# Conditional residual layer: W1 of the first eight batches loaded by id, and the row copies moved behind the first product

## The chip, the cores and the metric

The kernel runs on one core of one Trainium2 chip. The metric is device time in microseconds (us) of one execution. Before the change it is 313.89 us, the median of three runs (313.76 to 314.14). The trace used below is of one profiled execution, which took 313.83 us.

## The reference, cut to what matters

There are 128 batches of x, each 128 rows of 512 float32 values. Each batch has an integer id from 0 to 8 that picks one of ten sets of parameters.

```python
w1 = W1[ids]                 # (512, 128) per batch
w2 = W2[ids]                 # (128, 512) per batch
h = relu(einsum('bsh,bha->bsa', x, w1) + b1[ids][:, None, :])
y = x + einsum('bsa,bah->bsh', h, w2) + b2[ids][:, None, :]
out = x + layernorm(y) * gamma[ids][:, None, :] + beta[ids][:, None, :]
```

W1 is (10, 512, 128), W2 is (10, 128, 512); b1 is (10, 128), b2, gamma and beta are (10, 512).

## The kernel before, in words

One batch is one tile of 128 partitions by 512 columns. Four batches share one buffer of x (512 columns each, `xp`, four buffers). For each batch b:

- `transpose_x(b)` (L211, PE): four 128x128 transposes of x into one PSUM tile `pxT` (a single buffer); `copy_xT(b)` (L220, ACT) copies it to SBUF. For b below `EARLY` (16) the transposes read every fourth column of x, because the W1 that goes with them is laid out by `(p k)`; from batch 16 on they read 128 neighbouring columns.
- `stage_w1(b)` (L206, ACT): copies the 128x512 slice of W1 that belongs to the batch's id out of the whole table in SBUF (`w1e` for b below `EARLY`, `w1` after) into a small tile `w1s` (three buffers).
- `down(b)` (L237, PE): four products of `xT` and `w1s`, accumulated in one PSUM tile `ph` (a single buffer); `relu(b)` (L247, ACT) adds b1 and makes `hT`.
- `up(b)` (L251, PE): `hT` times the id's slice of `w2`, 128x512, into `py`; the first four batches and some later ones add b2 here by one more product. `py` shares five PSUM buffers with the `row` tiles of `spread`.
- On POOL `add_b2(b)` (L224) makes x + b2 and `add_beta(b)` (L230) makes x + beta, in buffers `r` (four) and `o` (five, two batches each). On DVE and ACT follow the residual with its sum, the squares, the deviation and its reciprocal, `scale` (L319) and `finish` (L327). `store` (L334) writes two batches of `o` at once.

Before the loop come the tables. The rows of beta, gamma and b2 (30 in all) are brought to all 128 partitions: `parts` on DVE (L153 to L157) splits them in three bf16 parts, and `spread(r, copier)` (L171) does for row r one bf16 product on PE into a `row` tile and one 128x512 copy into SBUF on ACT or DVE. In the kernel before, rows 0 to 19 are spread ahead of the first `down`, in between the transposes of batches 0 and 1, and rows 20 to 29 behind `down(0)` to `down(3)`. `spin` (L451) is PE work without use: eleven products at the start, one half-width product for every second row in `spread_turn`, three before the first `down`.

The order within every engine is the order in which the program text issues, because `keep` (L44) ties each instruction to the one before it on its engine. All loads and all stores but three small ones are issued from SP's queue, in this order before the loop: ids, gamma, x of batches 0 and 1, `w1e` in two halves (L102), x of 2 and 3, `w2` in two halves (L116), x of 4 and 5, x of 6 and 7, x of 8 to 11. In the loop (`for i in range(3, B + U)`, L492), turn i issues `transpose_x(i)`, `down(i-1)`, `copy_xT(i)`, `stage_w1(i+1)`, `relu(i-1)`, `up(i-2)`, then DVE's work on batch b = i-3. The second layout of W1 (`load_w1`, L109, rows of 512 bytes) is loaded in turns 4, 6, 8 and 10. Each DMA carries one of eight semaphores in turn, and waits until the DMA eight places earlier has landed.

The id is read from `lang`, a row of 128 clamped ids that DVE makes (L147 to L150): `lid(b, engine)` (L185) loads four of them into registers of an engine.

Of the kernel before, what the change touches and what calls it, by code (L numbers as in the profile page):

```python
# [8 lines left out]
FP = mybir.dt.float32  # L9
# [4 lines left out]
ET = mybir.EngineType  # L14
PSUM = bass.MemoryType.PSUM

P = 128
G = 4
EPS = 1e-5
EARLY = 16  # L20
U = 2


# [1 line left out]
def cond_resid_kernel(ctx: ExitStack, tc: tile.TileContext, x, itok, W1, b1, W2, b2, gamma, beta, out):  # L25
# [8 lines left out]
    nc = tc.nc  # L34
    B, S, H = x.shape
    L, _, A = W1.shape
    KC = H // P
# [6 lines left out]
    def keep(ins):  # L44

        engine = ins.ins.engine
        if engine in last:
            tc.add_manual_dep(ins.ins, last[engine], behind, reason="kept order")
        last[engine] = ins.ins.name
        return ins  # L50

    const = ctx.enter_context(tc.tile_pool(name="const", bufs=1))
    xp = ctx.enter_context(tc.tile_pool(name="xp", bufs=4))
    rp = ctx.enter_context(tc.tile_pool(name="rp", bufs=4))
    op = ctx.enter_context(tc.tile_pool(name="op", bufs=5))
    tp = ctx.enter_context(tc.tile_pool(name="tp", bufs=2))
    wp = ctx.enter_context(tc.tile_pool(name="wp", bufs=3))
    st = ctx.enter_context(tc.tile_pool(name="st", bufs=6))
    p_x = ctx.enter_context(tc.tile_pool(name="p_x", bufs=1, space=PSUM))
    p_h = ctx.enter_context(tc.tile_pool(name="p_h", bufs=1, space=PSUM))  # L60
# [3 lines left out]
    xs = {}  # L64

    def load_x(g):
        t = xp.tile([P, G, H], FP, tag="x", name=f"x_{g}")
        keep(nc.sync.dma_start(out=t, in_=x[g * G : (g + 1) * G].rearrange("b s h -> s b h")))
        xs[g] = t

    def xb(b):
        return xs[b // G][:, b % G, :]
# [6 lines left out]
    w1e = const.tile([P, L, KC, A], FP, name="w1e")  # L79
    w2 = const.tile([P, L * H], FP, name="w2")  # L80
# [3 lines left out]
    def load_part(lo, hi):  # L84
        dst = xs[lo // G][:, lo % G : lo % G + hi - lo, :]
        keep(nc.sync.dma_start(out=dst, in_=x[lo:hi].rearrange("b s h -> s b h")))
# [8 lines left out]
    warm = const.tile([P, 1], FP, name="warm")  # L95
    keep(nc.vector.memset(warm, 1.0))
    keep(nc.scalar.activation(warm, warm, AF.Sqrt))


    for l in range(0, L, 5):  # L100
        keep(
            nc.sync.dma_start(  # L102
                out=w1e[:, l : l + 5].rearrange("p l k a -> p l (k a)"),
                in_=W1[l : l + 5].rearrange("l (p k) a -> p l (k a)", k=KC),
            )
        )
    load_part(2, G)

    def load_w1(k):  # L109
        keep(  # L110
            nc.sync.dma_start(out=w1[:, :, k, :], in_=W1[:, k * P : (k + 1) * P, :].rearrange("l p a -> p l a"))
        )

    for l in range(0, L, 5):
        keep(
            nc.sync.dma_start(  # L116
                out=w2[:, l * H : (l + 5) * H].rearrange("p (l h) -> p l h", l=5),
                in_=W2[l : l + 5].rearrange("l a h -> a l h"),
            )
        )  # L120
    x_1 = xp.tile([P, G, H], FP, tag="x", name="x_1")
    xs[1] = x_1
    load_part(G, G + 2)
    load_part(G + 2, 2 * G)
    load_x(2)

    ident = const.tile([P, P], FP, name="ident")
    make_identity(nc, ident)
# [7 lines left out]
    R = 3 * L  # L136
# [5 lines left out]
    keep(nc.vector.tensor_tensor(pick, both, ident[:96, 64 : 64 + R], ALU.add))  # L142
    keep(nc.vector.tensor_scalar(pick[:, L : 2 * L], pick[:, L : 2 * L], 2.0, None, ALU.mult))


    wrap = const.tile([1, B], I32, name="wrap")
    keep(nc.vector.tensor_scalar(wrap, ids, 0, L, ALU.is_lt, ALU.mult))  # L147
    lang = const.tile([1, B], I32, name="lang")
    keep(nc.vector.tensor_tensor(lang, ids, wrap, ALU.add))
    keep(nc.vector.tensor_scalar(lang, lang, 0, L - 1, ALU.max, ALU.min))  # L150

    left = rp.tile([P, H], FP, tag="r", name="left")
    keep(nc.vector.tensor_copy(parts[0:R, :], rows[0:R, :]))  # L153
# [17 lines left out]
    def spread(r, copier):  # L171
        t = (beta_b, gamma_b, b2_b)[r // L]
        row = p_y.tile([P, H], FP, tag="y", name=f"row_{r}")
        pick_r = pick[:, r : r + 1].to_broadcast([96, P])
        keep(nc.tensor.matmul(row, lhsT=pick_r, rhs=parts[:96, :], start=True, stop=True))  # L175
        dst = t[:, r % L * H : (r % L + 1) * H]
        if copier is nc.scalar:
            keep(nc.scalar.copy(dst, row))  # L178
        else:
            keep(nc.vector.tensor_copy(dst, row))  # L180

    lids, xT, w1s, hT, rs, os, ys, ssqs, nmeans, rstds = {}, {}, {}, {}, {}, {}, {}, {}, {}, {}
    phs, pxs, sums = {}, {}, {}

    def lid(b, engine):  # L185
        g = b // G
        if (g, engine) not in lids:
            loads, vals = nc.values_load_multi_w_load_instructions(
                lang[0:1, g * G : (g + 1) * G],
                engines=[engine],  # L190
                min_val=0,
                max_val=L - 1,
                skip_runtime_bounds_check_because="clamped on the chip to 0..L-1 above",
            )
            for ins in loads:
                keep(ins)
            lids[g, engine] = vals
        return lids[g, engine][b % G]

    def b2_by_matmul(b):  # L200
        return b < 4 or (b % 4 == 1 and not b2_by_vector(b))
# [4 lines left out]
    def stage_w1(b):  # L206
        w1s[b] = wp.tile([P, KC, A], FP, tag="w1s", name=f"w1s_{b}")
        src = (w1e if b < EARLY else w1).rearrange("p l k a -> p (l k a)")[:, bass.ds(lid(b, ET.Activation) * (KC * A), KC * A)]
        keep(nc.scalar.copy(w1s[b].rearrange("p k a -> p (k a)"), src))  # L209

    def transpose_x(b):  # L211
        pxs[b] = p_x.tile([P, KC, P], FP, tag="xT", name=f"pxT_{b}")
        for k in range(KC):
            if b < EARLY:
                cols = xb(b).rearrange("s (p k) -> s k p", k=KC)[:, k, :]
# [122 lines left out]
    def on(b):  # L338
        return 0 <= b < B
# [111 lines left out]
    def spin(n, width):  # L451
        idle = p_s.tile([P, H], FP, tag="s", name="idle")
        for _ in range(n):
            keep(
                nc.tensor.matmul(
                    idle[:, :width], lhsT=ones, rhs=ones[:, 0:1].to_broadcast([P, width]), start=True, stop=True
                )
            )


    def spread_turn(lo, hi):
        for r in range(lo, hi):
            spread(r, nc.scalar if r % 2 == 1 else nc.vector)
            if r % 2 == 1:
                spin(1, H // 2)

    spin(11, H)
    spread_turn(0, 2)
    transpose_x(0)
    transpose_b1()  # L470
    copy_xT(0)
    spread_turn(2, 8)
    transpose_x(1)
    copy_xT(1)
    spread_turn(8, 20)
    stage_w1(0)
    stage_w1(1)
    spin(3, H)
    for b in range(4):
        down(b)  # L480
        if b < 2:
            transpose_x(b + 2)
        relu(b)
        if b < 2:
            copy_xT(b + 2)
        for r in range(20 + 3 * b, min(23 + 3 * b, R)):
            spread(r, nc.scalar if r % 3 == 1 else nc.vector)
        stage_w1(b + 2)
    up(0)
    up(1)  # L490

    for i in range(3, B + U):  # L492
        b = i - U - 1
        if b > 0 and b % G == 0 and b // G + 3 < NG:
            load_x(b // G + 3)
        if i == 5:
            load_x(3)
        if i in (4, 6, 8, 10):
            load_w1((i - 4) // 2)
        if i == 4:  # L500
            up(2)
        if i == 5:
            up(3)
        if i > 3 and on(i):
            transpose_x(i)
        if b <= E:
            add_b2(b + 2)
            add_beta(b)
        if i > 4 and on(i - 1):
            down(i - 1)  # L510
        if i > 3 and on(i):
            copy_xT(i)
        if i > 4 and on(i + 1):
            stage_w1(i + 1)
        if i > 4 and on(i - 1):
            relu(i - 1)
        if i > 5 and on(i - U):
            up(i - U)


        g, half = divmod(b, 2)
        p = g - 1
        mine, old = 0 <= p < B // 2, 0 <= p - 1 < B // 2
        if b == E:
            add_b2(b + 3)
            add_beta(b + 1)
            add_b2(b + 4)
            for n in range(b + 2, B):
                add_beta(n)
        if b > E:  # L530
            tail(b)
        elif half == 0:
            if on(b):
                residual(b)
            if mine:
                rstd_1(p)
                scale(2 * p)
            if on(b):
                negative_mean(b)
            if mine:  # L540
                rstd_2(p)
            if old:
                finish(2 * p - 1)
                store(p - 1)
            if mine:
                rstd_3(p)
        else:
            if on(b):
                residual(b)
            if mine:  # L550
                rstd_4(p)
                scale(2 * p + 1)
            if on(b):
                negative_mean(b)
            if mine:
                finish(2 * p)
        if 0 <= b <= E:
            square(b)
            if half == 1:
                deviation(g)  # L560

        for n, engine in ((i + 3, ET.Activation), (i - U + 3, ET.PE), (b + 1, ET.DVE), (b + 5, ET.Pool)):
            if on(n):
                lid(n, engine)
# [37 lines left out]
```

## Time and profile before

| what | value |
|---|---|
| median of three runs | 313.89 us |
| the profiled execution | 313.83 us |
| span of its trace | 312.1 us |
| PE, DVE, ACT, POOL busy in the span | 300.5, 297.3, 285.4, 280.1 us |
| first `down` starts | 14.04 us |
| last product ends | about 302.3 us |
| moved by DMA | 75.49 MB, mean 242 GB/s |

The span is the time from the first to the last recorded instruction; 1.73 us of the execution lie around it. In a timeline each line has a start, a length, the engine, the line of the program, the operation with the tile written and the tile read, and how many instructions were merged; a bracket gives the idle time of the engine before it and what ended it. In a table of windows each engine has its busy time in that stretch and the number of its instructions, then come the clock granted to PE, the share of the DMA engines and what they moved. The chain of waits is followed back from the last instruction, each step to what released it.

### The profile page before, as it was taken

The page shows a single profiled execution, that of the slowest core. Times are in us where ns is not written, and L with a number is a line of the kernel's source. Part 1 is how long each engine was busy: PE and PEld are TensorE (multiplying, and loading weights), DVE is VectorE, ACT ScalarE, POOL GpSimd, SP SyncE. Part 2 cuts the span into 40 slices and gives each one's busy share as a digit, 9 for nine tenths or more (in the row PEclk, how much of TensorE's full clock was granted, in tenths as well). Part 3 has the DMA queues.
Part 4 walks back from the last instruction along what each step waited for, and adds up shares of the span by engine and source line. Part 5 has one row for each costly group of instructions (what it writes and reads, how often), then busy time and mean ns, then how long its engine had stood idle before and what let it go on. Part 6 is the DMA issues. An engine that isn't in the chain of part 4 may idle for free.

```text
span 312.1 us, 7096 instructions
## 1 busy us (share of the span) xinstructions
PE 300.5 (96%) x1869; PEld 223.8 (72%) x1869; DVE 297.3 (95%) x945; ACT 285.4 (91%) x724; POOL 280.1 (90%) x234
## 2 busy tenths in 40 slices
PE   8999999999999999999999999999999999999970
PEld 3567787777777767777777777777777777777740
DVE  6677999999999999999999999999999999999995
ACT  3878999999999999999999999999999999999982
POOL 1319978999999999999999999999999999999963
PEclk9999999999999999999999999999999999999995
DMA  6999998767776777667666567576666667633234
GB/s 209 387 387 352 326 339 275 238 229 226 236 250 225 255 265 269 242 231 270 257 227 226 210 238 253 213 272 269 232 232 198 232 247 239 244 134 138 88 149 168
DMA packets 42313, 75.49 MB, mean 242 GB/s; under 512 B 1785, under 2 KB 6916, under 8 KB 42274
## 3 DMA queue, kind: packets, MB, share of 16 engines
q1 hardware_dynamic: 42214, 75.00, 68.6%
q8 instruction: 15, 0.25, 0.3%
q14 instruction: 24, 0.20, 0.2%
q10 hardware_dynamic: 60, 0.05, 0.1%
HBM read 41.49 MB, written 33.55 MB: 240 GB/s over the span
## 4 chain that ended last, share of the span: by engine, by line
PE 91%; DVE 5%; ACT 1%; issue 1%; DVEq 1%; DMA 1%; ACTq 0%
PE ph L241 36%; PE py L258 34%; PE pxT L218 18%; PE py L257 1%; PE row L175 1%; DVE py L273 1%; DVE gamma_b L180 1%; DVE py L322 1%; DVE o L331 1%; DMA rows<-in_L_cond_b_dram 1%; ACT sq L366 0%; DVEq L597 0%; ACT n L382 0%; DVE left L156 0%; DVE left L154 0%
## 5 line engine op out<-in xcount | busy, mean ns | idle before, releaser
L235 POOL TENSOR_TENSOR o<-x,beta_b 128x512 f32<-128x512 f32 x128 | 161.6, 1274 | 12.8 <-ACT beta_b L178 9.2
L241 PE MATMUL ph<-xT,w1s 128*128 128x128 f32 x1024 | 135.6, 275 | 0.5 <-ACT w1s L209 0.5
L258 PE MATMUL py<-w,hT 128*128 x256 | 131.1, 594 | 0.0
L228 POOL TENSOR_TENSOR r<-x,b_b 128x512 f32<-128x512 f32 x93 | 118.5, 1274 | 11.5 <-DMA x<-in_x_dram 9.2
L241 PEld LDWEIGHTS ph<-xT,w1s 128*128 128x128 f32 x1024 | 124.7, 192 | 2.4 <-ACT w1s L209 1.0
L218 PEld LDWEIGHTS pxT<-ident,x 128*128 128x128 f32 x512 | 65.5, 148 | 64.9 <-issue 44.8
L322 DVE SCALAR_TENSOR_TENSOR py<-py,nmean,gamma_b 128x512 f32<-128x512 f32 x126 | 93.8, 745 | 0.2 <-issue 0.2
L331 DVE SCALAR_TENSOR_TENSOR o<-py,rstd,o 128x512 f32<-128x512 f32 x122 | 91.0, 746 | 0.0
L288 ACT ACTIVATE sq<-py,sum 128x512 f32<-128x512 f32 x124 | 85.3, 688 | 1.4 <-DVE py L273 1.3
L222 ACT COPY xT<-pxT 128x512 f32<-128x512 f32 x128 | 73.8, 577 | 9.8 <-PE pxT L218 6.3
L218 PE MATMUL pxT<-ident,x 128*128 128x128 f32 x512 | 77.4, 274 | 0.0
L209 ACT COPY w1s<-w 128x512 f32 x112 | 69.5, 621 | 0.0
L273 DVE SCALAR_TENSOR_TENSOR py<-py,r 128x512 f32<-128x512 f32 x93 | 64.6, 694 | 1.3 <-PE pxT L218 0.6
L249 ACT ACTIVATE hT<-ph,b1T 128x128 f32<-128x128 f32 x128 | 47.4, 370 | 1.0 <-PE ph L241 1.0
L258 PEld LDWEIGHTS py<-w,hT 128*128 128x128 f32 x256 | 40.6, 192 | 2.4 <-ACT hT L249 0.7
L273 DVE SCALAR_TENSOR_TENSOR py<-py,x 128x512 f32<-128x512 f32 x35 | 24.4, 697 | 1.6 <-ACT sq L288 0.6
L288 ACT ACTIVATION_READ_ACCUMULATOR sq<-py,sum 128x1 f32 x124 | 25.7, 208 | 0.0
L299 ACT ACTIVATE sd<-ssq,eps 128x2 f32<-128x2 f32 x62 | 18.3, 296 | 2.1
L279 DVE TENSOR_SCALAR nmean<-sum 128x1 f32<-128x1 f32 x128 | 19.5, 152 | 0.1
L305 DVE RECIPROCAL stat<-sd 128x2 f32<-128x2 f32 x62 | 13.0, 210 | 1.0 <-ACT sd L299 1.0
L273 DVE DVE_READ_ACCUMULATOR py<-py,r 128x1 f32 x93 | 13.4, 144 | 0.0
L317 DVE RECIPROCAL rstd<-stat 128x2 f32<-128x2 f32 x62 | 10.4, 168 | 0.0
(56 smaller groups left out, 120.6 us busy)
## 6 DMA issues: line engine op xcount, KB each, us to landing
out_dram<-o SPq DMA_DIRECT2D x61, 512.0 KB, 3.9
x<-in_x_dram SPq DMA_DIRECT2D x30, 1024.0 KB, 5.8
w1e<-in_L_cond_W_dram SPq DMA_DIRECT2D x2, 1280.0 KB, 8.7
w<-in_L_cond_W_dram SPq DMA_DIRECT2D x2, 1280.0 KB
w<-in_L_cond_W_dram SPq DMA_DIRECT2D x4, 640.0 KB, 15.2
x<-in_x_dram SPq DMA_DIRECT2D x4, 512.0 KB, 8.4
out_dram<-o SPq DMA_DIRECT2D x6, 256.0 KB, 2.0
rows<-in_L_cond_beta_dram ACTq DMA_DIRECT2D x1, 20.0 KB
```

Of the source, the lines that this page charges most:

```text
L209: keep(nc.scalar.copy(w1s[b].rearrange("p k a -> p (k a)"), src))
L218: keep(nc.tensor.transpose(pxs[b][:, k, :], cols, ident))
L222: keep(nc.scalar.copy(xT[b], pxs.pop(b)))
L228: keep(nc.gpsimd.tensor_tensor(rs[b], xb(b), b2_b[:, bass.ds(v * H, H)], ALU.add))
L235: keep(nc.gpsimd.tensor_tensor(os[g][:, j, :], xb(b), beta_b[:, bass.ds(v * H, H)], ALU.add))
L241: nc.tensor.matmul(phs[b], lhsT=w1s[b][:, k, :], rhs=xT[b][:, k, :], start=(k == 0), stop=(k == KC - 1))
L249: keep(nc.scalar.activation(hT[b], phs.pop(b), AF.Relu, bias=b1T[:, bass.ds(lid(b, ET.Activation), 1)]))
L258: keep(nc.tensor.matmul(ys[b], lhsT=hT[b], rhs=w2[:, bass.ds(v * H, H)], start=not m, stop=True))
L273: nc.vector.scalar_tensor_tensor(ys[b], ys[b], 1.0, r, ALU.mult, ALU.add, accum_out=col(sums, b))
L288: nc.scalar.activation(sq, ys[b], AF.Square, bias=col(sums, b), scale=-float(H), accum_out=col(ssqs, b))
L322: nc.vector.scalar_tensor_tensor(ys[b], ys[b], col(nmeans, b), gamma_b[:, bass.ds(v * H, H)], ALU.add, ALU.mult)
L331: nc.vector.scalar_tensor_tensor(o, ys.pop(b), rstds[g][:, j : j + 1], o, ALU.mult, ALU.add)
```

## The change

1. W1 of batches 0 to 7 is loaded for each batch alone: `load_first(b)` reads the id into a register of SP and issues a 128x512 load (262,144 bytes) from W1 at that id straight into `w1s`. `wp` has five buffers in place of three. `stage_w1` now begins with batch 8.
2. SP's order before the loop is now: ids, gamma, x of 0 and 1, the register load, W1 for 0, W1 for 1, x of 2 and 3, W1 for 2, W1 for 3, `w2` in two halves, x of 4 and 5, W1 for 4 and 5, x of 6 and 7, W1 for 6 and 7, `w1e` in two halves, x of 8 and 9, x of 10 and 11.
3. `EARLY` is 28: `w1e` and the transposes of every fourth column serve batches up to 27. `load_w1` moves to turns 8, 10, 12 and 14.
4. Only rows 0 and 1 are spread ahead of `down(0)`, behind the transposes of batches 0 and 1. Behind `down(0)`, `down(1)`, `down(2)` and `down(3)` come seven rows each. Three rows of seven go to ACT, four to DVE. The spins within `spread_turn` and the three ahead of the first `down` are gone; the eleven at the start stay.

```diff
-EARLY = 16
+FIRST = 8
+EARLY = 28
...
-    wp = ctx.enter_context(tc.tile_pool(name="wp", bufs=3))
+    wp = ctx.enter_context(tc.tile_pool(name="wp", bufs=5))
...
+    def load_first(b):
+        w1s[b] = wp.tile([P, KC, A], FP, tag="w1s", name=f"w1s_{b}")
+        src = W1[bass.ds(lid(b, ET.SP), 1)].rearrange("o (p k) a -> p (o k a)", k=KC)
+        keep(nc.sync.dma_start(out=w1s[b].rearrange("p k a -> p (k a)"), in_=src))
+
+    load_first(0)
+    load_first(1)
+    load_part(2, G)
+    load_first(2)
+    load_first(3)
+    for l in range(0, L, 5):
+        keep(
+            nc.sync.dma_start(
+                out=w2[:, l * H : (l + 5) * H].rearrange("p (l h) -> p l h", l=5),
+                in_=W2[l : l + 5].rearrange("l a h -> a l h"),
+            )
+        )
+    x_1 = xp.tile([P, G, H], FP, tag="x", name="x_1")
+    xs[1] = x_1
+    for b in (G, G + 2):
+        load_part(b, b + 2)
+        load_first(b)
+        load_first(b + 1)
+    for l in range(0, L, 5):
+        keep(
+            nc.sync.dma_start(
+                out=w1e[:, l : l + 5].rearrange("p l k a -> p l (k a)"),
+                in_=W1[l : l + 5].rearrange("l (p k) a -> p l (k a)", k=KC),
+            )
+        )
+    x_2 = xp.tile([P, G, H], FP, tag="x", name="x_2")
+    xs[2] = x_2
+    load_part(2 * G, 2 * G + 2)
+    load_part(2 * G + 2, 3 * G)
...
-    def spread_turn(lo, hi):
-        for r in range(lo, hi):
-            spread(r, nc.scalar if r % 2 == 1 else nc.vector)
-            if r % 2 == 1:
-                spin(1, H // 2)
-
     spin(11, H)
-    spread_turn(0, 2)
     transpose_x(0)
     transpose_b1()
     copy_xT(0)
-    spread_turn(2, 8)
     transpose_x(1)
     copy_xT(1)
-    spread_turn(8, 20)
-    stage_w1(0)
-    stage_w1(1)
-    spin(3, H)
+    turns = (0, 2, 9, 16, 23, R)
+
+    def spread_turn(n):
+        for r in range(turns[n], turns[n + 1]):
+            spread(r, nc.scalar if r % 7 in (1, 3, 5) else nc.vector)
+
+    spread_turn(0)
     for b in range(4):
         down(b)
         if b < 2:
...
-        for r in range(20 + 3 * b, min(23 + 3 * b, R)):
-            spread(r, nc.scalar if r % 3 == 1 else nc.vector)
-        stage_w1(b + 2)
+        spread_turn(b + 1)
     up(0)
     up(1)
...
-        if i in (4, 6, 8, 10):
-            load_w1((i - 4) // 2)
+        if i in (8, 10, 12, 14):
+            load_w1((i - 8) // 2)
...
-        if i > 4 and on(i + 1):
+        if i + 1 >= FIRST and on(i + 1):
             stage_w1(i + 1)
```

The loads of `w1e` and of x for 8 to 11 that stood earlier in the text are taken out there, and `lid` is moved up unchanged.

More of the change, by code (lines that the diff above doesn't have):

```diff
@@ L97, in cond_resid_kernel @@
     keep(nc.scalar.activation(warm, warm, AF.Sqrt))
[L100 to L107, printed above, removed]
     def load_w1(k):
@@ L112, in load_w1 @@
         )
[L114 to L125, printed above, removed]
     ident = const.tile([P, P], FP, name="ident")
@@ L143, in cond_resid_kernel @@
     keep(nc.vector.tensor_scalar(pick[:, L : 2 * L], pick[:, L : 2 * L], 2.0, None, ALU.mult))
+    lids, w1s = {}, {}
     wrap = const.tile([1, B], I32, name="wrap")
@@ L150, in cond_resid_kernel, with lid @@
     keep(nc.vector.tensor_scalar(lang, lang, 0, L - 1, ALU.max, ALU.min))
+    def lid(b, engine):
+        g = b // G
+        if (g, engine) not in lids:
+            loads, vals = nc.values_load_multi_w_load_instructions(
+                lang[0:1, g * G : (g + 1) * G],
+                engines=[engine],
+                min_val=0,
+                max_val=L - 1,
+                skip_runtime_bounds_check_because="clamped on the chip to 0..L-1 above",
+            )
+            for ins in loads:
+                keep(ins)
+            lids[g, engine] = vals
+        return lids[g, engine][b % G]
+    def load_first(b):
[26 more added lines that the diff above has]
+            )
+        )
+    x_2 = xp.tile([P, G, H], FP, tag="x", name="x_2")
+    xs[2] = x_2
+    load_part(2 * G, 2 * G + 2)
+    load_part(2 * G + 2, 3 * G)
     left = rp.tile([P, H], FP, tag="r", name="left")
@@ L180, in spread @@
             keep(nc.vector.tensor_copy(dst, row))
-    lids, xT, w1s, hT, rs, os, ys, ssqs, nmeans, rstds = {}, {}, {}, {}, {}, {}, {}, {}, {}, {}
+    xT, hT, rs, os, ys, ssqs, nmeans, rstds = {}, {}, {}, {}, {}, {}, {}, {}
     phs, pxs, sums = {}, {}, {}
[L185 to L198, printed above, removed]
     def b2_by_matmul(b):
```

## The prediction

> **What bounds the kernel now.** I read the chain of waits first:
>
> ```profile
> PE 91%; DVE 5%; ACT 1%; issue 1%; DVEq 1%; DMA 1%; ACTq 0%
> ```
>
> PE's own work is 91% of the path. The timeline shows `down(4)` starting at 26.27, `down(8)` at 34.88, `down(12)` at 43.98: from there PE never starves and takes about 2.2 us a batch to the end. A change in the first 26 us is thus worth the shift of this steady train. Second, what holds the train's start, from the timeline:
>
> ```profile
> 1.50 0.41 SPq L86 DMA_DIRECT2D x<-in_x_dram  x1
> 2.61 0.21 DVE L150 TENSOR_SCALAR lang<-lang 1x128 int32<-1x128 int32 x1
> 5.41 0.42 DVE L157 CAST parts<-left 30x512 bf16<-30x512 f32 x1
> 10.30 3.07 DVE L180 COPY gamma_b<-row 128x512 f32<-128x512 f32 x5
> 10.46 2.76 ACT L178 COPY gamma_b<-row 128x512 f32<-128x512 f32 x5
> 13.37 1.14 ACT L209 COPY w1s<-w1e 128x512 f32 x2 [0.15 <-DVE gamma_b L180]
> 14.04 1.16 PE L241 MATMUL ph<-xT,w1s 128*128 128x128 f32 x8 [0.47 <-ACT w1s L209]
> 21.24 1.02 PE L258 MATMUL py<-w,hT 128*128 x2
> 22.33 1.27 POOL L228 TENSOR_TENSOR r<-x,b_b 128x512 f32<-128x512 f32 x1 [9.21 <-DMA x<-in_x_dram]
> 26.27 1.06 PE L241 MATMUL ph<-xT,w1s 128*128 128x128 f32 x8
> 32.19 0.63 PE L218 MATMUL pxT<-ident,x 128*128 128x128 f32 x4
> ```
>
> The reader sees that row copies take 0.61 us each on DVE (3.07/5) and 0.55 on ACT (2.76/5), that `down(0)` waits for them and two W1 copies until 14.04, that the first `up` follows at 21.2, and that transposes of batch 8 run at 32.19. Third, the table of windows, whose last column is what DMA moved:
>
> ```profile
> 0.00:5.00 5.00, 3.82 (x10) 1.32 (x11) 3.36 (x12) 1.49 (x2) 0.88 (x8) 1.00 0.51 148
> 5.00:10.00 5.00, 4.92 (x28) 2.89 (x27) 3.85 (x8) 3.38 (x7) 0.00 (x0) 1.00 1.00 344
> 10.00:15.00 5.00, 4.47 (x26) 2.51 (x25) 3.38 (x6) 4.36 (x9) 2.49 (x2) 1.00 1.04 393
> 15.00:20.00 5.00, 5.00 (x36) 3.89 (x36) 3.08 (x5) 4.36 (x10) 0.00 (x0) 1.00 1.05 389
> 20.00:25.00 5.00, 5.00 (x24) 3.12 (x24) 3.43 (x10) 2.73 (x7) 2.67 (x3) 1.00 1.05 386
> ```
>
> From 5 us on DMA is full at about 389 GB/s. Summed up, 0.74 MB have moved by 5 us, 2.46 by 10, 4.43 by 15, 6.37 by 20, 8.30 by 25. Against SP's order (0.07 MB of rows, x of two batches 0.52, each table 2.62) this gives landings: the first half of `w1e` is recorded as landing 7.1 us after its issue at 1.95, so at 9.05, when 2.13 MB had moved against 1.90 due. So a load lands when the sum up to its end plus 0.23 MB has moved, some 0.65 us behind its place in line.
>
> **The Trainium skill.** "DMA: Bandwidth & Descriptors", Queues, rings and completion order: every DMA engine consumes a ring's descriptors in order, so a load waits for the bytes ahead of it. The trace agrees (the 0.23 MB lag above). The same page, Latency and other measured facts, puts the floor of a register load at about 600 ns; the trace has 0.30 to 0.92 us on other engines and none on SP. "TensorE: Matmul & The Clock Gate", Part 1: the array runs at half clock until it has been busy for a window of some 3.4 us, and falls back after an idle one. The trace shows it in spacing: eleven spins take 4.62 us (0.42 each), later three 512-wide row products take 0.81 with their latency. "SBUF — State Buffer", Door 1: lines are 16 bytes, and a read that crosses to a new one for each element pays; every fourth float32 does. Trace: from `down(13)` to `down(14)` it is 2.22 us, from `down(14)` to `down(15)`, with the first transposes of neighbouring columns, 2.19.
>
> **The change part by part.**
>
> *The first product.* `lang` is ready at 2.82. A register load on SP, taken as 0.9 (bounds 0.3 and 1.0), puts the issue of the first W1 at about 3.75. Data moves about 1.3 us after an issue (x at 1.50, bytes in quantity from 2.8), so W1 moves from 5.0, with a small hole behind x. At 344 GB/s 0.26 MB takes 0.8, plus 0.65: landed at 6.5. On PE the spins last to 5.8; transposes of batch 0 to 6.44, ACT's copy to 7.06, transposes of batch 1 at 7.1, rows 0 and 1 at 7.55, `down(0)` at about 8.0 in place of 14.04. The two W1 copies (1.14) leave the path; all eight leave ACT.
>
> *The rows.* 28 rows now lie behind `down(0)`, 10 before. DVE copies four per turn (2.4 us), ACT three (1.6) with its relu (0.35) and `xT` copy (0.55), so 2.5 us a turn; PE has 0.9 + 0.45 + 7 x 0.22 = 2.9, the last two turns 2.45. With five PSUM buffers I followed each row: transposes of batch 2 need x at about 8.8 (below), then `down(1)` at 11.2, `down(2)` 14.2, `down(3)` 16.6; DVE ends row 25 at 19.2, and its buffer is what `up(0)` needs: 19.2, against 21.02 for its b2 product now. Gain 1.8. From there to batch 8's transposes are 11.17 us of PE work (32.19 - 21.02), unchanged: 30.4. POOL's first `r` needs all of b2, done at 20.4, two us before today's 22.33.
>
> *The loads.* Sum from 5.0 at 344, from 10 at 389, each plus 0.65: x of 2 and 3 done at 8.05, lands 8.7; W1 of 2 and 3 10.2; `w2` 17.0 (`up(0)` wants it at 19.4); x of 4 and 5 18.3; W1 of 4, 5 19.7; x of 6, 7 21; W1 of 6, 7 22.4; `w1e` 29.1; x of 8 and 9 at 30.5. Now x of 8 to 11 has 8.45 MB in front of its end; the change puts 10.0 in front of batch 9's: the eight loads repeat 2.1 MB that `w1e` brings again. ACT wants `w1e` for batch 8 as its `w1s` copy comes, 31.15 today, 29.3 after: covered by 0.2. PE wants batch 8 at 30.4, it lands at 30.5: the 6 us of slack are gone, and 1 us of delay here costs 1 us. Gain at this point 32.19 - 30.5 = 1.7.
>
> *Waits on SP.* W1 of 5, 6 and 7 reuse buffers and wait for `down(0)` to `down(2)` (15.1). SP would reach the last at about 11.5, as today it issues some 8.5 us ahead of the data; then 3 MB are queued, to 21 us. The wait costs nothing while the queue holds; behind it stand `w1e` and all x from 8 on, which would be late by whatever the queue ran dry. x of 12 to 15 lands at about 34.5, wanted at 39. The first store then lands at about 38.5, before now 34.45 + 8.6 = 43.1; POOL waited 2.25 for it, so POOL gains. Turns 8 to 14 for the second W1 layout: wanted only from turn 27, free.
>
> *`EARLY` 28.* Twelve more batches at 0.03 us: +0.36, on PE's path with nothing to hide it.
>
> *Spins gone.* They gave nothing to the path; as cover for the clock they count. Taken as 0, since PE stays some 75% busy; bounds 0 and +6 (two turns at half clock, 3 us each). Nothing is below 0.
>
> Sum: -1.7 + 0.36 = -1.34, so 313.83 - 1.34 = 312.5; the profiled run is 0.06 below the median, which changes nothing.
>
> **Rivals.**
>
> *A, more gain:* loads run at the 400 GB/s of the best stretches and rows pace better; PE reaches batch 8 at 29.5. Gain 2.7 - 0.36: 311.5. For: copies alone would let `up(0)` start a us earlier. Against: two turns are tight on PE too.
>
> *B, nothing left:* x of 2 and 3, or batch 8, lands about 1.1 us later than reckoned (a slower start of SP, as rates of 3 to 8 us are uneven). Gain 0.6 - 0.36: 313.6, no change. For: both loads are reckoned to within 0.2 us of their need.
>
> *C, slower:* the eight single loads cost more than their bytes. Place: DMA's queue up to x of 8 and 9. Price: 0.35 us of lost time each, 2.8 in all, so batch 8 at 33.3, 1.1 later than now, + 0.36: 315.3. It decides from 1.3 us in all (0.16 a load), where landing passes 31.8. For: no load of this form by a register is in the trace, and SP needs about 0.45 to issue one that lasts 0.67. Against: the queue holds far more than one load.
>
> *D, clock:* without spins PE falls to half clock within the row turns: +6, less what is spare, about 317. Against: idle stretches there are below 1 us each.
>
> **How the numbers follow.** Forecast 312.5 with chance 0.40, own range 311.9 to 313.1; A 0.12, B 0.20, C 0.20, D 0.08. A measurement here tells 0.2%, 0.63 us, from no change. Faster: forecast and A, 0.52. Same: B, 0.20. Slower: C and D, 0.28. The range leaves out D, the far half of C and a little of A: 311.3 to 315.4.
>
> **What would show it.** `down(0)` near 8.0, `up(0)` near 19.2, POOL's first `r` near 20.5, transposes of batch 8 near 30.5 with their wait put down to x, steps of 2.22 up to batch 27. Wrong if batch 8 starts past 31.8, if row products space 0.43 in place of 0.22, or if PE is idle between 30 and 45 us.

## The result, and the profile after

| | before | after |
|---|---|---|
| median, 20 executions each (us) | 313.92 | 314.51 |
| lowest and highest | 313.63, 314.27 | 314.18, 315.93 |
| the profiled execution, and its span | 313.83, 312.1 | 314.31, 312.6 |

The ratio of after to before is 1.0027, with a 95% interval of 1.0018 to 1.0036. The change costs about 0.6 us; the forecast was a gain of 1.3 us. Further down, every ratio is to the kernel before, run in the same session; its median there was 313.77 to 313.79 us.

The timeline of the kernel after, in the columns of the one shown before:

```profile
8.61 1.05 PE L258 MATMUL ph<-xT,w1s 128*128 128x128 f32 x8
...
20.02 0.10 PEld L274 LDWEIGHTS <-pick 96*128 x1 [0.63 <-issue]
20.12 0.38 PE L274 MATMUL py<-parts,pick 96*128 96x512 bf16 x1 [0.24 <-issue]
...
21.05 1.26 POOL L245 TENSOR_TENSOR r<-x,b_b 128x512 f32<-128x512 f32 x1 [4.36 <-DVE b_b L212]
...
31.24 0.62 ACT L226 COPY w1s<-w1e 128x512 f32 x1 [1.16 <-DMA w1e<-in_L_cond_W_dram]
...
32.56 1.28 POOL L245 TENSOR_TENSOR r<-x,b_b 128x512 f32<-128x512 f32 x1 [2.85 <-DMA x<-in_x_dram]
...
32.63 0.72 PE L235 MATMUL pxT<-ident,x 128*128 128x128 f32 x4 [1.20 <-DMA x<-in_x_dram]
33.18 1.06 PE L258 MATMUL ph<-xT,w1s 128*128 128x128 f32 x8
```

The start did become early: the first product runs at 8.6 us instead of 14.0, and the first `up` (its b2 product) at 20.12 instead of 21.02. Then three engines stop at once between 30 and 33 us. ACT waits 1.16 us for `w1e`, POOL 2.85 us for x of batch 8, and PE 1.20 us for the same x. Its transposes run at 32.63, against 32.19 before. The product at 33.18 is `down(7)`, whose turn they stand in; its weight load starts at 33.07.

The chain of waits of the kernel after, shares by engine and the head of the shares by line:

```profile
PE 83%; DMA 8%; DVE 4%; SPq 1%; issue 1%; ACT 1%; DVEq 1%; POOL 0%; ACTq 0%; POOLq 0%
...
PE ph L258 33%; PE py L275 32%; PE pxT L235 17%; DMA x<-in_x_dram 8%; PE py L274 1%; DVE py L290 1%; DVE py L339 1%; DVE o L348 1%; SPq L152 1%; ACT sq L383 0%; DVEq L607 0%; SPq L161 0%; ACT n L399 0%; DVE o L410 0%; DVEq L134 0%
```

DMA's share of the path has gone from 1% to 8%, and all of it stands beside x. Followed back from the end, the path runs through PE to batch 8's transposes, and from there into the queue of loads instead of into PE's own start. There it goes through two loads of x: that of batches 8 and 9, issued at 19.30 and landed at 32.5, and that of batches 4 and 5, issued at 7.05 and landed at 19.30, whose semaphore SP waited for before it issued the later one. The products, row copies and activations ahead of 32.6 us no longer set the time.

The same by batch, as the start of the first weight load of each `down` in the two traces:

| `down(b)` | before | after | difference |
|---|---|---|---|
| 0 | 14.04 | 8.40 | -5.64 |
| 3 | 19.81 | 16.91 | -2.90 |
| 6 | 30.10 | 29.17 | -0.93 |
| 7 | 32.54 | 33.07 | +0.53 |
| 15 | 50.51 | 51.05 | +0.54 |
| 28 | 79.42 | 80.30 | +0.88 |
| 127 | 298.98 | 299.48 | +0.50 |

Two steps are plain: 1.46 us lost at batch 8, and 0.34 us between batches 15 and 28. The fall from 0.88 to 0.50 is mostly two single steps in the trace of before, at batches 43 and 73, that took 0.2 us longer there than in the trace of after. No part of the change touches them, and why they were long stays open.

The table of windows of the kernel after (columns as before: PE, PEld, DVE, ACT, POOL busy with their instructions, clock, DMA share, GB/s):

```profile
0.00:5.00 5.00, 3.81 (x9) 1.34 (x10) 3.27 (x12) 1.49 (x2) 0.88 (x8) 1.00 0.44 129
5.00:10.00 5.00, 4.53 (x27) 3.46 (x26) 1.71 (x4) 1.96 (x4) 0.00 (x0) 1.00 0.95 309
10.00:15.00 5.00, 5.00 (x33) 3.34 (x31) 4.13 (x7) 4.37 (x10) 0.80 (x1) 1.00 1.03 353
15.00:20.00 5.00, 4.83 (x28) 2.65 (x26) 4.89 (x9) 3.87 (x9) 1.69 (x2) 1.00 1.05 388
20.00:25.00 5.00, 4.88 (x17) 2.59 (x18) 3.46 (x10) 2.13 (x5) 3.94 (x4) 1.00 1.05 388
25.00:30.00 5.00, 5.00 (x38) 4.43 (x37) 4.12 (x15) 4.51 (x13) 4.71 (x4) 1.00 1.04 385
30.00:35.00 5.00, 3.80 (x22) 2.48 (x21) 3.53 (x11) 3.25 (x9) 2.44 (x2) 1.00 1.05 386
```

The last column times 5 us, added up, gives 3.96 MB by 15 us. Before had moved 4.43 MB by then, though after must bring more. From 15 us on after runs at 385 to 388 GB/s, and before ran at 386 to 389 up to 25 us, so what was lost early was not made up ahead of batch 8. The clock column is 1.00 throughout.

### The profile page after: what moved, and what is told of

Its sections match the earlier page's. It is cut to its first block, busy times and chain, and to the rows that moved or that the text cites. A ratio compares the mean times of both kernels' runs of the same rounds, so it can differ in the third digit from the quotient of the medians.

```text
span 312.6 us, 7094 instructions
## 1 busy us (share of the span) xinstructions
PE 299.7 (96%) x1856; PEld 224.2 (72%) x1856; DVE 297.3 (95%) x945; ACT 281.0 (90%) x716; POOL 280.3 (90%) x234
## 4 chain that ended last, share of the span: by engine, by line
PE 83%; DMA 8%; DVE 4%; SPq 1%; issue 1%; ACT 1%; DVEq 1%; POOL 0%; ACTq 0%; POOLq 0%
PE ph L258 33%; PE py L275 32%; PE pxT L235 17%; DMA x<-in_x_dram 8%; PE py L274 1%; DVE py L290 1%; DVE py L339 1%; DVE o L348 1%; SPq L152 1%; ACT sq L383 0%; DVEq L607 0%; SPq L161 0%; ACT n L399 0%; DVE o L410 0%; DVEq L134 0%
## 5 line engine op out<-in xcount | busy, mean ns | idle before, releaser
L235 PEld LDWEIGHTS pxT<-ident,x 128*128 128x128 f32 x512 | 67.5, 154 | 66.2 <-issue 45.0
L239 ACT COPY xT<-pxT 128x512 f32<-128x512 f32 x128 | 73.7, 576 | 15.2 <-PE pxT L235 11.2
L235 PE MATMUL pxT<-ident,x 128*128 128x128 f32 x512 | 78.4, 276 | 1.7 <-DMA x<-in_x_dram 1.2
L226 ACT COPY w1s<-w 128x512 f32 x100 | 62.0, 620 | 0.0
L226 ACT COPY w1s<-w1e 128x512 f32 x20 | 12.4, 620 | 1.2 <-DMA w1e<-in_L_cond_W_dram 1.2
## 6 DMA issues: line engine op xcount, KB each, us to landing
w1e<-in_L_cond_W_dram SPq DMA_DIRECT2D x2, 1280.0 KB, 13.2
```

Of the source, the lines that this page charges most:

```text
L235: keep(nc.tensor.transpose(pxs[b][:, k, :], cols, ident))
L239: keep(nc.scalar.copy(xT[b], pxs.pop(b)))
```

## The experiments

The account to be tested has two parts. First, x of batch 8 stands behind too many bytes in SP's queue, because the eight loads by id repeat what `w1e` brings again; its landing sets the time from there on. Second, each of the batches 16 to 27 pays for transposes of every fourth column. The main rival to the first is that SP, waiting for the buffers of W1 5 to 7 or for a semaphore, issues `w1e` and x too late. The rival to the second is that DMA traffic slows those batches. Where expectations number their theories, the first is this account and the second the rival; rival 3 is that the low rate early in the queue belongs to the loads by id themselves, and theory 4 is about a register load on PE.

In what follows, landing of x of batch 8 is read where POOL and PE wait for it, and differences of a `down` are against the trace of before unless another kernel is named.

**The transposes of every fourth column alone.** The kernel before with one number changed:

```diff
-EARLY = 16
+EARLY = 28
```

> The kernel before with EARLY = 28 alone. Theory 1 (transposes of every fourth column cost PE 0.03 us a batch on the path): steps from one down to the next of 2.22 us up to batch 27, so 12 x 0.03 = 0.36 us more, about 314.3 against 313.9. Rival (the 0.03 us between batches 15 and 16 is some effect of the DMA traffic of that stretch, not of the columns): steps fall to 2.19 from batch 16 on as before, and the time stays at 313.9.

Measured: 314.14 us against 313.79 of before on the same chip, ratio 1.0011 (1.0005 to 1.0018). In the trace the difference is 0.03 us up to `down(14)`, grows by 0.03 us a batch to 0.38 at `down(27)`, and stands still from there to `down(34)`. That is 0.35 us, the same as in the kernel after over the same batches, with none of the new loads in it. The second part holds, and its rival falls.

**Fewer bytes in front of batch 8.** The kernel after, with `w1e` holding six of the ten sets of W1: 1.05 MB fewer. It doesn't compute the same: batches 8 to 27 take W1 at half the offset, so other weights than the reference's.

```diff
-    w1e = const.tile([P, L, KC, A], FP, name="w1e")
+    w1e = const.tile([P, 6, KC, A], FP, name="w1e")
...
-    for l in range(0, L, 5):
+    for l in range(0, 6, 3):
...
+        step = KC * A // 2 if b < EARLY else KC * A
```

> The changed kernel with w1e of six languages in place of ten (1.05 MB fewer); batches 8 to 27 take W1 at half the offset and so multiply with other weights than the reference. Theory 1 (bytes ahead of batch 8): 1.05 MB at 0.388 MB per us are 2.7 us, so x of batch 8 lands at 29.8, before PE wants it; down(7) near 31.6 and the time near 313.1. Rival 2 (SP's waits for buffers): the bytes matter little, down(7) at 32.5 or later, the time at 314 or more.

Measured: 313.18 us, ratio 0.9981 (0.9970 to 0.9993). Timeline of this kernel around batch 8 (lines stand one lower in the program):

```profile
30.12 1.29 POOL L246 TENSOR_TENSOR r<-x,b_b 128x512 f32<-128x512 f32 x1
30.42 0.62 ACT L227 COPY w1s<-w1e 128x512 f32 x1
...
31.71 0.63 PE L236 MATMUL pxT<-ident,x 128*128 128x128 f32 x4
```

None of the three lines carries a bracket that names a DMA: all three waits are gone. The transposes run at 31.71, as soon as PE comes to them. SP issued x of 8 to 11 no earlier than in after; its line in the kernel after, then in this one:

```profile
19.30 3.59 SPq L87 DMA_DIRECT2D x<-in_x_dram  x2
19.32 1.03 SPq L87 DMA_DIRECT2D x<-in_x_dram  x2
```

Issued at the same time, x of batch 8 had landed by 30.12, when POOL read it without a wait, at least 2.4 us earlier than in after. So it isn't the time of issue that made it late, and the wait for a semaphore falls as a cause. `down(7)` is 0.48 us earlier than before instead of 0.53 later, and all later batches keep that, less the 0.35 us of the transposes. Only bytes ahead of x were taken away, and of the 1.46 us nothing is lost any more: `down(7)` has the same lead as `down(5)` and `down(6)`. The first part holds.

**The buffers that SP waits for, first attempt.** The kernel after, with the W1 of the first eight batches in slots of the empty table `w1` instead of the five buffers, so that SP waits for none:

```diff
-        w1s[b] = wp.tile([P, KC, A], FP, tag="w1s", name=f"w1s_{b}")
+        w1s[b] = w1[:, b]
```

> The changed kernel with the eight single loads written into the still empty table w1 in place of w1s, so that none of them waits for a product to free its buffer. Theory 1 (batch 8 is late because of the bytes queued ahead of it): down(7) stays near 33.1, the time near 314.5, within 0.2 us. Rival 2 (SP stands at W1 of batches 5 to 7 until down(0) to down(2) have ended, and w1e and x behind them start late): x of batch 8 lands up to 1.4 us earlier, down(7) near 31.6, the time near 313.1.

Measured: 325.92 us, ratio 1.0397 (1.0380 to 1.0414). This kernel didn't do what it was made for. The first part of the second W1 layout is issued in turn 8, ahead of `down(7)` in the text, into the table that holds slot 7. It writes over a quarter of that slot with the other layout, so `down(7)` took other weights than the reference's, and it waited until 42.27 for that load. Its time says nothing of SP. Up to batch 6 it can be used: SP issued `w1e` at 14.83 instead of 16.00, yet x of batch 8 landed at 32.40 instead of 32.56.

**The same, mended.** The second layout moves one turn later, behind `down(7)`:

```diff
-        if i in (8, 10, 12, 14):
-            load_w1((i - 8) // 2)
+        if i in (9, 11, 13, 15):
+            load_w1((i - 9) // 2)
```

> As the run with the eight single loads in the empty table w1, but with the loads of the second layout moved from turns 8 to 14 to turns 9 to 15: there the first of them stood ahead of the product of batch 7 and wrote over its slot, so that its whole time tells nothing. Theory 1 (bytes queued ahead of batch 8): down(7) near 33.0 and the time within 0.3 us of the changed kernel, 314.5. Rival 2 (SP waits for buffers): down(7) near 31.6, 313.1. In the run before, x of batch 8 landed 0.16 us earlier than in the changed kernel, which speaks for theory 1.

Measured: 314.34 us, ratio 1.0024 (1.0014 to 1.0034), the same as after. Its timeline:

```profile
31.18 0.62 ACT L226 COPY w1s<-w1e 128x512 f32 x1 [0.29 <-DMA w1e<-in_L_cond_W_dram]
...
32.54 1.28 POOL L245 TENSOR_TENSOR r<-x,b_b 128x512 f32<-128x512 f32 x1 [2.00 <-DMA x<-in_x_dram]
```

x of batch 8 landed within 0.02 us of after's 32.56, without one wait for a buffer of W1. SP issued `w1e` at 14.79 instead of 16.00, and x of 8 and 9 at 19.53, not before after's 19.30. So the buffers of W1 delay the issue of `w1e` by 1.2 us, but neither its landing, read on ACT at 31.18 and 31.24, nor x, and this rival falls. There is a second reading in this run: its first rows lagged, and `down(4)` came at 26.15, 0.8 us later than in after (25.33). `down(7)` was at 33.04 all the same, against 33.07. Eight tenths of a microsecond of lead on PE are worth nothing while the landing decides.

**No `w1e` at all.** The kernel after with `FIRST` and `EARLY` at 16: W1 of 16 batches by id, in twelve buffers, and the second layout from batch 16 on. The 2.62 MB of `w1e` leave the queue, and nothing takes their place ahead of x of 8 and 9; batches 16 to 27 transpose neighbouring columns again.

```diff
-FIRST = 8
-EARLY = 28
+FIRST = 16
+EARLY = 16
...
-    wp = ctx.enter_context(tc.tile_pool(name="wp", bufs=5))
+    wp = ctx.enter_context(tc.tile_pool(name="wp", bufs=12))
...
-    load_part(2 * G, 2 * G + 2)
-    load_part(2 * G + 2, 3 * G)
+    for b in (2 * G, 2 * G + 2):
+        load_part(b, b + 2)
+        load_first(b)
+        load_first(b + 1)
...
+            for n in range(12, FIRST):
+                load_first(n)
-        if i in (8, 10, 12, 14):
-            load_w1((i - 8) // 2)
+        if i in (5, 6, 7, 8):
+            load_w1(i - 5)
```

> The changed kernel without w1e: W1 of the first 16 batches is loaded by id (FIRST = EARLY = 16, twelve buffers), the second layout of W1 is loaded in turns 5 to 8. Theory 1: 2.1 MB fewer ahead of batch 8, no wait there, no twelve extra strided batches: down(7) near 31.6, about 313.0, unless the second layout of W1 lands after 47 us; then up to 315 with a wait of ACT for it before batch 16. Rival 2 (SP's waits): here no load before batch 12 waits for a buffer either, so also about 313; this run tells what is left to gain, not which of the two.

Measured: 313.20 us, ratio 0.9984 (0.9972 to 0.9996). `down(4)` is 0.60 us earlier than before, `down(7)` 0.72, and the lead stays 0.72 through batch 28: neither the loss at batch 8 nor that of the fourth columns is there. The lead itself is small, though `down(0)` ran at 7.04, because in this execution the transposes of batch 2 then waited 1.33 us for x of 2 and 3, until 9.64. The traces of the six sets (1.45 us) and of the slots (1.34 and 1.17) have this wait too. The trace of after has not: there PE came to these transposes later, at 9.50, behind a `down(0)` at 8.40.

**The early hole.** In after, x of 2 and 3 is issued at 4.50, behind the register load and two loads of W1. Here it is issued right after x of 0 and 1, and nothing else is changed:

```diff
     load_part(0, 2)
+    load_part(2, G)
...
     load_first(0)
     load_first(1)
-    load_part(2, G)
     load_first(2)
```

> The changed kernel with x of batches 2 and 3 issued right behind x of 0 and 1, ahead of the register load on SP. Theory 1, second part (between 4 and 5 us DMA has little queued, because SP waits for the id and its register load): the hole fills, some 0.2 MB are moved earlier, x of batch 8 lands 0.5 us earlier, the transposes of batch 2 don't wait; about 314.0. Rival 3 (the low rate of the first 10 us belongs to the loads by id themselves): the rate stays low, less than 0.2 us gained.

Windows of one microsecond, of the kernel after:

```profile
3.00:4.00 1.00, 1.00 (x4) 0.32 (x3) 0.84 (x2) 0.56 (x2) 0.00 (x0) 1.00 0.92 345
4.00:5.00 1.00, 1.00 (x3) 0.30 (x2) 0.93 (x3) 0.00 (x0) 0.00 (x0) 1.00 0.63 170
```

and of this kernel:

```profile
3.00:4.00 1.00, 1.00 (x4) 0.32 (x3) 0.87 (x2) 0.57 (x2) 0.00 (x0) 1.00 0.95 351
4.00:5.00 1.00, 1.00 (x3) 0.30 (x2) 0.93 (x3) 0.00 (x0) 0.00 (x0) 1.00 1.03 399
```

The hole between 4 and 5 us is filled, with 0.23 MB more, 0.6 us at 387 GB/s. By 15 us this kernel has moved 4.37 MB (178, 313 and 382 GB/s in the windows of 5 us), 0.40 more than after; most of the rest came between 10 and 15 us, and why is open. This kernel's timeline at batch 8:

```profile
30.26 0.62 ACT L226 COPY w1s<-w1e 128x512 f32 x1 [1.04 <-DMA w1e<-in_L_cond_W_dram]
...
31.57 1.28 POOL L245 TENSOR_TENSOR r<-x,b_b 128x512 f32<-128x512 f32 x1 [2.70 <-DMA x<-in_x_dram]
...
31.64 0.72 PE L235 MATMUL pxT<-ident,x 128*128 128x128 f32 x4 [1.07 <-DMA x<-in_x_dram]
```

x lands 0.99 us earlier, twice what was expected, and the three waits are still there: the path is still the queue, and what is moved early in it comes out at its end. Measured: 313.55 us, ratio 0.9993 (0.9985 to 1.0001), so 1 us of DMA in the first 15 us took back the whole loss against before.

**Both, and PE's register load moved.** With the edit of x on top of the kernel without `w1e`:

> The version without w1e (16 batches by id) with x of 2 and 3 issued ahead of the register load. There nothing waits at batch 8, so a gain in the start shows in full. Theory 1: transposes of batch 2 stop waiting for x (1.33 us in the trace of that version), down(1) at about 11.0 in place of 11.6, up(0) 0.5 earlier: 312.6 against 313.2. Rival 3 (low rate belongs to the loads by id): W1 of batch 0 lands later by the 0.5 MB now ahead of it, down(0) moves from 7.0 to about 8.3, and the time stays within 0.2 us.

Measured: 312.54 us, ratio 0.9954 (0.9939 to 0.9969). The transposes of batch 2 don't wait for x, and the lead is 1.03 us from `down(5)` to `down(34)`. `down(0)` was at 8.30, as rival 3 had it, but not by its cause: W1 of batch 0 landed at 7.0, and the time went down by 0.66 us. The first transposes were slow in this execution (0.97 us; see the end). PE's timeline at the first `up` of this kernel:

```profile
19.91 0.10 PEld L268 LDWEIGHTS <-pick 96*128 x1 [0.62 <-issue]
20.02 0.38 PE L268 MATMUL py<-parts,pick 96*128 96x512 bf16 x1 [0.23 <-issue]
```

The 0.62 us put down to "issue" is the same gap as in after (0.63). No tile is waited for: PE's sequencer loads four ids into registers there, for the slice of `w2` (PE's first such load starts at 19.2 in this trace), and no product is queued meanwhile. The last run moves that load ahead of the last seven row products:

```diff
+        if b == 3:
+            lid(0, ET.PE)
         spread_turn(b + 1)
```

> As the last, and PE reads the ids of batches 0 to 3 into its registers ahead of the last seven row products in place of behind them. Theory 4 (the first up is late by 0.6 us because PE's sequencer loads registers while nothing is queued, the 0.63 us ahead of the first up that the trace puts down to issue): another 0.3 to 0.5 us, 312.2. Rival (the copy that frees the buffer is late anyway): no change against the last run.

```profile
19.16 0.10 PEld L268 LDWEIGHTS <-pick 96*128 x1
19.54 0.38 PE L268 MATMUL py<-parts,pick 96*128 96x512 bf16 x1
```

The gap is gone, the product comes at 19.54 instead of 20.02, and from `down(5)` on every batch is 0.49 us earlier than in the run above. Not all of that is the edit's: `down(0)` to `down(3)`, ahead of it, are already 0.13 us earlier, with first transposes of 0.83 us instead of 0.97. The move itself is worth 0.35 us in these traces, as expected. What keeps the rest of the 0.62 us isn't shown; the rival's late copy may be part of it. Measured: 311.52 us (311.23 to 312.00), ratio 0.9924 (0.9911 to 0.9937). The medians of the two, of six and five executions, differ by 1.02 us, of which this explains a third; the rest isn't explained. This is the best of the versions run, 0.8% under the kernel before.

## Why the prediction was wrong

**The step that failed is "The loads".** It had `w1e` landing at 29.1 and x of 8 and 9 at 30.5. They landed at about 31.2 and 32.5. The mechanism was seen: it says that PE's wait at batch 8 would be put down to x, and that "1 us of delay here costs 1 us". The size was off by 2.0 us, and its own signs of being wrong, batch 8 past 31.8 and PE idle between 30 and 45 us, both came. The 2.0 us have two terms:

- The rate at the start. The step took 344 GB/s from 5 to 10 us and 389 from there, the rates of the kernel before, on top of the 0.59 MB that stand ahead of the first W1; that is 4.26 MB by 15 us. The windows after add up to 3.96 MB. The 0.30 MB are 0.8 us at 387 GB/s. SP waits for the id, and DMA has a hole from 4 to 5 us; with x of 2 and 3 issued ahead of that wait, batch 8 came forward by 0.99 us.
- The lag behind the place in line. One landing, at 9 us, gave 0.23 MB, and this was used for all. x of 8 and 9 has 10.03 MB up to its end in the queue, and 10.73 MB had moved by 32.5 us: 0.7 MB, or 1.8 us at 387 GB/s. That is 1.2 us more than the 0.65 us used. Another trace agrees: with x of 2 and 3 first, 10.78 MB had moved at 31.57, a lag of 0.75 MB.

The second term could have been read before the change. These are the bytes moved by 32.5 us in after, then, of the kernel before, the load of x of 6 and 7 (issued at 11.73, 13.2 us to its landing at 24.93) and the bytes moved by then:

```profile
DMA packets 5566, 10.73 MB, mean 330 GB/s; under 512 B 328, under 2 KB 339, under 8 KB 5565
...
x<-in_x_dram SPq DMA_DIRECT2D x1, 512.0 KB, 13.2
...
DMA packets 4209, 8.27 MB, mean 332 GB/s; under 512 B 169, under 2 KB 180, under 8 KB 4208
```

Up to the end of that x 7.41 MB were due, so the lag was 0.86 MB already then. With it, and its own rates, the step would have put x of 8 and 9 at about 32.1 (an estimate).

So "Gain at this point 32.19 - 30.5 = 1.7" became a loss of 0.44 at batch 8's transposes. The time is what rival B's mechanism gives with twice its delay, or what rival C gives at the same place with less than its price. C's own cause, 0.35 us of lost time for each single load and 2.8 in all, isn't what the traces show: with x of 2 and 3 first, the kernel with the same eight loads had moved 4.37 MB by 15 us against 4.43 before, 0.06 MB or 0.2 us less. Four of the eight lie in those bytes by their place in the queue; the other four move after 15 us, where it runs at 387 to 389 GB/s. Dips do remain between 6 and 11 us in all these kernels (195 GB/s from 10 to 11 us in after, from 8 to 9 with the hole filled), where before has no such microsecond under 330 GB/s; their cause is open.

**The first product: right but for 0.4 to 0.6 us.** SP's first W1 went out at 3.53 (reckoned 3.75), 0.74 us after `lang` was ready, so the register load was no dearer than thought. (The range of such loads was misread: in the trace of before they take up to 1.35 us, not 0.92.) `down(0)` came at 8.4 to 8.6 instead of 8.0, mostly since the transposes of batch 0 took 1.06 us there and not 0.63.

**The rows: the second step that failed.** `down(1)`, `down(2)` and `down(3)` at 11.36, 14.32 and 16.91 stand beside 11.2, 14.2 and 16.6. The first `up` at 20.12 doesn't: 19.2 was reckoned. The gain was 0.90 and not 1.8; 0.3 of the difference was there at `down(3)`, and 0.6 is the gap at the register load on PE, which the step didn't have. Before shows no such gap: the row product and the b2 product follow each other at 20.80 and 21.02. It cost nothing in after, where the queue decides, but 0.35 us in the last pair of runs, where it doesn't. The shortfall matters for the forecast too. In after PE came to batch 8's transposes at 31.43, 1.20 us ahead of x, and not at 30.4. Had x landed as reckoned, the gain there would have been 0.76 us and not 1.7, less 0.35 for `EARLY`: about 313.4 (an estimate), again outside the range. So this step failed as well, hidden behind the first.

**Waits on SP: right.** Taking the waits for buffers away moved the landing by 0.02 us. The second W1 layout was in time too: from `down(28)` to `down(34)` the difference stays within 0.01 us. x of 12 to 15 landed at 36.5 and not 34.5, the same 2.0 us late.

**`EARLY` 28: right.** 0.36 was forecast, 0.35 measured, in the kernel after and alone.

**Spins gone: right for the rows.** The seven row products behind `down(0)` took 1.76 us together, about 0.23 apart and not 0.43; rival D's +6 us did not come. POOL's first `r` came at 21.05 (reckoned 20.5), and POOL set nothing until x of batch 8.

**Rival A fell** with the rate: from 15 us on the loads ran at 385 to 388 GB/s and not at 400.

The wider spread of after, up to 315.93 us against 314.27, isn't explained. It is not the new path alone: the versions with six sets and without `w1e`, where nothing waits at batch 8, reach 315.43 and 315.39 us. The three versions with x of 2 and 3 ahead of the register load stay at or below 314.15 us in their 24 executions. What ties the spread to that order was not tried.

## What to carry to other kernels

When a start is pulled forward, follow the loads to the first consumer behind the new bytes, and price the landing there by what lagged in that part of the queue, not by one early landing. A gain on an engine is only worth what the next late transfer leaves of it: here 5.6 us at the first product were 0.9 at the seventh batch and less than nothing at the ninth. Where such a landing decides, bytes loaded twice and holes in the queue while an id is awaited come out at its end; a better change takes the second copy out and puts loads that need no id in the hole.

## What the runs showed of the hardware

- A load's lag behind its place in one long queue was not a constant: in before 0.23 MB at 9 us and 0.86 MB at 24.9 us, in after 0.36 MB for `w2` (4.79 MB due, 5.15 moved when it landed at about 18.1 us) and 0.7 MB at 32.5 us. The order itself is as the Trainium skill has it ("DMA: Bandwidth & Descriptors", Queues, rings and completion order): 1.05 MB taken out ahead of x brought x forward by at least 2.4 us at the same time of issue. Why the lag grows was not tried.
- A register load on PE showed as 0.62 to 0.63 us of "issue" when nothing was queued on PE; placed ahead of queued products the gap vanished. The floor of about 600 ns that the same page gives (Latency and other measured facts) isn't what these traces show. In after the median of PE's 32 loads is 0.33 us, and SP's first, ahead of W1, took 0.49 us:

```profile
L134 PEldq TENSOR_LOAD <-lang x32: 328/332/801, 19.3 to 288.9; - x32
L134 SPq TENSOR_LOAD <-lang x2: 309/400/491, 2.8 to 8.7; - x2
```

  In these lines stand the shortest, the median and the longest load in ns, then when the first and the last began.
- Transposes of every fourth float32 column cost 0.03 us for four 128x128 blocks, all of it on PE's path.
- The first four transposes took 1.06 us in the profiled execution of after and 0.97 in the one without `w1e` and with x of 2 and 3 first, but 0.63 with x of 2 and 3 first alone, at a clock column of 1.00 in all. So that column did not show what slowed them, and `down(0)` lies anywhere from 7.04 to 8.40 in traces of kernels that start alike, for causes that no run separates.
